# A decoder layer on one core: latent attention weights turned by 32x32 blocks on VectorE, and values times weights in tiles of 32 rows

## The chip, the core and the metric

The kernel runs on one core of a Trainium2 chip. The metric is device time in microseconds from launch to end, the median of several executions. Engines are named as the profile names them: PE is TensorE (PEld its weight loads), DVE is VectorE, ACT is ScalarE, POOL is GpSimd, SP is SyncE, whose queue issues nearly all DMAs here.

## What is computed

32 sequences of 256 tokens with 256 channels pass through one decoder layer, all in float32:

```python
x = layernorm(x + latent_attention(x))
x = layernorm(x + cross_attention(x, ctx))     # 16 heads of 64, 120 context rows
x = layernorm(x + experts(x) + shared(x))      # 16 experts, 32 tokens each, and a shared one

def latent_attention(x):                       # H = 16 heads, L = 72 latent columns
    kv = x @ latent_w + latent_b               # [b, 256, 72]: keys and values of every head
    q = einsum('btc,hcl->bhtl', x, Wd_w) + Wd_b
    scores = einsum('bhtl,bsl->bhts', q, kv) / sqrt(16)
    attn = softmax(where(causal, scores, -inf))
    y = einsum('bhts,bsl->bhtl', attn, kv)     # the product that the change is about
    return concat_heads(y) @ out_w + out_b     # 16 * 72 = 1152 columns into 256
```

Attention is causal: of 256 x 256 weights per head, the upper right quarter of 128 x 128 is never computed.

## The kernel before

The 32 sequences run one behind the other, as a pipeline written out by hand: `first_half(n)` and `second_half(n)` hold steps of sequence n (latent scores of four groups of four heads), n-1 (the weighting, `latent_out`, cross attention) and n-2, n-3 (the rest of cross attention, the routing). For n from 1 on, the order on PE and ACT is the order in which the code calls the steps; DVE, POOL and SP are ordered by the planner, which gives steps inside `urgent()` precedence. The last sequence overlaps the feed-forward part, which follows and whose steps come from a generator (`fill`).

The steps around the change, for group g of four heads:

- `scores` makes four PSUM tiles `pS` of 128 x 384: token block 0 against keys 0 to 127, and token block 1 against keys 0 to 255. The 72 latent columns are taken as 64 (row tiles of 64, L442) and 8 (row tiles of 32, L430). DVE adds the mask (L451) into `sm`.
- `weights` is the softmax in place: DVE maximum (L464), ACT exponent (L467), DVE reciprocal, POOL product (L475).
- `turn` transposes `sm` on PE (L489) in three blocks of 128 per head, 48 per sequence, into a PSUM tile `pT`; DVE (L493) or ACT (L495) copies it to `pt0` and `pt1`.
- `weigh` (L509) multiplies the 64 first value columns (the stationary operand, column tiles of 64, two heads side by side) with the turned weights, once per group, into `pz`; `weigh_rest` (L530) does the same with the last 8 columns, spread to 32, in column tiles of 32 (four heads side by side) for all groups into one `pzr`.
- Copies bring them to `zT`, nine chunks of 128 rows; `latent_out` multiplies these with `ow_sb` (18 matmuls of 256 columns, `po`), adds the residual and normalizes.

PSUM is eight banks: two with the tag "l" for cross scores and six with the tag "r" for all else, given out in rotation; a step that takes a bank waits until the copy out of its last use is done. An f32 matmul shows as two weight loads and two passes in the profile.

Of the kernel before, what the change touches and what calls it, by code (L numbers as in the profile page):

```python
# [26 lines left out]
P = 128  # L27
# [5 lines left out]
def decoder_kernel(  # L33
# [34 lines left out]
    HG = 4  # L68
# [10 lines left out]
    LR = L - LM  # L79
    QW = P // BQ  # L80
# [14 lines left out]

    mask = const.tile([P, 3 * P], F32, name="mask")
    nc.gpsimd.memset(mask, 0.0)
    for b in (0, 2):
        nc.gpsimd.affine_select(
            out=mask[:, b * P : (b + 1) * P],  # L100
            in_=mask[:, b * P : (b + 1) * P],
            compare_op=ALU.is_ge,
            fill=NEG,
            base=0,
            pattern=[[-1, P]],
            channel_multiplier=1,
        )
# [20 lines left out]

    VW = LM + NG * (32 + LR)

# [40 lines left out]
    def transposed(dst, src, name):  # L173

        turned = bank("r", [P, DC, T], name)
        for d in range(DC):
            for t in range(TC):
                nc.tensor.transpose(
                    turned[:, d, t * P : (t + 1) * P], src[:, t, d * P : (d + 1) * P], ident
                )  # L180
        with urgent():
            nc.vector.tensor_copy(dst, turned)
# [51 lines left out]
    v_bufs = [wp.tile([P, TC, VW], F32, name=f"v_{k}") for k in range(2)]  # L234
    for vb in v_bufs:
        nc.gpsimd.memset(vb, 0.0)
# [69 lines left out]
    def out_weights(part):  # L306
# [6 lines left out]
        for h in range(part * H // 2, (part + 1) * H // 2):  # L313
            lo = (h % HG) * 32 + (h // HG) * LR
# [16 lines left out]

    def load_context(m):
# [6 lines left out]
    def turn_x(s):  # L339
        st = states[s]  # L340
        st["xT"] = sp.tile([P, DC, T], F32, tag="xT", name=f"xT_{st['nm']}")
        transposed(st["xT"], st["x"], f"pxT_{st['nm']}")
# [20 lines left out]
    def values(s):  # L363
# [7 lines left out]
        v = v_bufs[s % 2]  # L371
        with urgent():
            nc.vector.tensor_copy(v[:, :, 0:LM], pv[:, :, 0:LM])
            nc.vector.tensor_copy(
                v[:, :, LM:].rearrange("p t (g k) -> p t g k", g=NG)[:, :, :, 0:LR],
                pv[:, :, LM:L].unsqueeze(2).to_broadcast([P, TC, NG, LR]),
            )
        st["v"] = v
# [98 lines left out]
    def turn(s, g, k):  # L477


        st = states[s]  # L480
        nm = f"{st['nm']}_{g}_{k}"
        if k == 0:
            st["pt0", g] = sp.tile([P, HG, TC, P], F32, tag="pt0", bufs=NG, name=f"pt0_{nm}")
        if k == 2:
            st["pt1", g] = sp.tile([P, HG, P], F32, tag="pt1", bufs=NG, name=f"pt1_{nm}")
        pT = bank("r", [P, HG, P], f"pT_{nm}")
        for j in range(HG):
            block = st["sm", g][:, j, k * P : (k + 1) * P]
            nc.tensor.transpose(pT[:, j, :], block, ident)  # L489
        dst = st["pt1", g] if k == 2 else st["pt0", g][:, :, k, :]  # L490
        with urgent():
            if k == 1:
                nc.vector.tensor_copy(dst, pT)  # L493
            else:
                nc.scalar.copy(dst, pT)  # L495

    def moving(st, g, j, k):
        return st["pt1", g][:, j, :] if k else st["pt0", g][:, j].rearrange("p t q -> p (t q)")

    def weigh(s, g):  # L500

        st = states[s]
        if g == 0:
            st["zT"] = sp.tile([P, ZC, T], F32, tag="zT", bufs=1, name=f"zT_{st['nm']}")
        pz = bank("r", [P, HG // 2, T], f"pz_{st['nm']}_{g}")
        for a in range(HG // 2):
            for k in range(TC):
                for odd in range(2):
                    nc.tensor.matmul(  # L509
                        pz[odd * LM : (odd + 1) * LM, a, k * P :],  # L510
                        st["v"][:, k, 0:LM],
                        moving(st, g, 2 * a + odd, k),
                        start=(k == 0),
                        stop=(k == TC - 1),
                    )
        dst = st["zT"][:, 2 * g : 2 * g + 2, :]
        with urgent():
            if g % 2:
                nc.vector.tensor_copy(dst, pz)
            else:  # L520
                nc.scalar.copy(dst, pz)

    def weigh_rest(s):

        st = states[s]
        pzr = bank("r", [P, T], f"pzr_{st['nm']}")
        for g in range(NG):
            for k in range(TC):
                for j in range(HG):
                    nc.tensor.matmul(  # L530
                        pzr[j * 32 : (j + 1) * 32, k * P :],
                        st["v"][:, k, LM + 32 * g : LM + 32 * (g + 1)],
                        moving(st, g, j, k),
                        start=(g == 0 and k == 0),
                        stop=(g == NG - 1 and k == TC - 1),
                    )
        with urgent():
            nc.scalar.copy(st["zT"][:, ZC - 1, :], pzr)

    def latent_out(s):  # L540
        st = states[s]
        po = bank("r", [P, TC, C], f"po_{st['nm']}")
        for t in range(TC):
            project(
                po[:, t, :],
                [(st["zT"][:, c, t * P : (t + 1) * P], ow_sb[:, c, :]) for c in range(ZC)],
            )
        r1 = ap.tile([P, TC, C], F32, tag="r", name=f"r1_{st['nm']}")
# [5 lines left out]
    def turn_x1(s):  # L554
        st = states[s]
        st["x1T"] = ap.tile([P, DC, T], F32, tag="xnT", bufs=1, name=f"x1T_{st['nm']}")
        transposed(st["x1T"], st["x1"], f"px1T_{st['nm']}")
# [3 lines left out]
    def cross_keys(m, n):  # L561

        pair = pairs[m]
        kxT = ap.tile([P, 4, 2, S2], F32, tag=f"kxT{n}", bufs=1, name=f"kxT_{m}_{n}")
# [743 lines left out]
```

## Time and profile before

| | |
|---|---|
| median of 3 runs | 3392.89 us (3392.28 to 3395.72) |
| the profiled execution | 3392.11 us, span of its instructions 3390.3 us |
| PE busy | 3368.9 us, 99% of the span |
| DVE, ACT, POOL busy | 1538.1, 1502.3, 1070.3 us |
| 800 to 1800 us (attention): DVE, ACT, POOL busy | 540, 564, 306 us of 1000 |
| granted PE clock | 1.00 |

Busy time of PE counts pipelined matmuls with their tails, so that 99% does not mean an array at its peak; the distance between the starts of two groups is what a group takes from the stream. A row of a group reads: line, engine, operation, written tile <- read tiles, shapes, count | busy us, mean ns of one | idle time before them and what ended it.

### The profile page before, as it was taken

The numbers are of one execution on the slowest core, as the hardware profiler recorded it, in microseconds if no ns is written. First come the engines' busy times: TensorE is split into PE (matmuls) and PEld (weight loads), VectorE is DVE, ScalarE is ACT, GpSimd is POOL, SyncE is SP. The second block draws the span as 40 slices with busy tenths as digits, with TensorE's granted clock in tenths as the row PEclk, the third lists the DMA queues.
The fourth block names the chain that finished last, engine by engine and source line by source line (L and its number), as shares of the span: only waits on it lengthen the run. The fifth ranks groups of instructions, "written<-read, shape, count | busy, mean of one in ns | idle before, by whom it ended". The sixth has DMA issues, their size and how long they took to land.

```text
span 3390.3 us, 59258 instructions
## 1 busy us (share of the span) xinstructions
PE 3368.9 (99%) x23020; PEld 2558.0 (75%) x23020; DVE 1538.1 (45%) x3416; ACT 1502.3 (44%) x5461; POOL 1070.3 (32%) x947
## 2 busy tenths in 40 slices
PE   9999999999999999999999999999999999999999
PEld 7788888888888888888888788887666655666655
DVE  4555555555555555555554655553322133121133
ACT  4656555555555555555555555564311111111111
POOL 3333333232322323232323223233444401444400
PEclk9999999999999999999999999999999999999999
DMA  3000000000000000000000000003455521555421
GB/s 99 11 17 26 15 22 18 17 19 22 21 18 19 19 16 25 18 21 19 15 20 15 27 17 21 16 12 111 108 124 124 135 90 57 122 124 123 103 86 47
DMA packets 142880, 164.50 MB, mean 49 GB/s; under 512 B 29448, under 2 KB 118536, under 8 KB 142600
## 3 DMA queue, kind: packets, MB, share of 16 engines
q1 hardware_dynamic: 117808, 126.08, 12.0%
q0 software_dynamic: 24576, 34.62, 5.7%
q8 instruction: 183, 3.00, 0.4%
q14 instruction: 97, 0.79, 0.1%
q10 hardware_dynamic: 216, 0.01, 0.0%
HBM read 105.61 MB, written 50.86 MB: 46 GB/s over the span
## 4 chain that ended last, share of the span: by engine, by line
PE 96%; DVE 2%; ACT 2%; POOL 0%; issue 0%; DMA 0%; SPq 0%; POOLq 0%; DVEq 0%; ACTq 0%
PE po L188 13%; PE pq L188 7%; PE pqx L188 7%; PE pd L188 7%; PE pu L188 6%; PE pg L188 6%; PE pS L442 5%; PE pz L509 5%; PE pT L489 5%; PE pc L667 3%; PE pu_s L188 3%; PE pg_s L188 3%; PE pL L625 3%; PE pfo L188 3%; PE pS L430 3%; PE pkx L188 3%
## 5 line engine op out<-in xcount | busy, mean ns | idle before, releaser
L475 POOL TENSOR_TENSOR sm<-sm,rs 128x512 f32<-128x512 f32 (+1 forms) x256 | 375.3, 1466 | 455.2 <-DVE rs L474 447.4
L467 ACT ACTIVATE sm<-sm,nmax 128x128 f32<-128x128 f32 (+1 forms) x1024 | 453.7, 462 | 89.2 <-DVE nmax L464 89.2
L475 POOL TENSOR_TENSOR xsm_x<-xsm_x,rs_x 128x480 f32<-128x480 f32 x256 | 252.1, 986 | 735.8 <-DVE rs_x L474 714.7
L467 ACT ACTIVATE xsm_x<-pL,nmax_x 128x120 f32<-128x120 f32 x1024 | 354.3, 375 | 13.2 <-DVE mv L160 10.2
L1082 POOL DMA_INDIRECT acc<-eo,offs x128 | 200.7, 1568 | 336.1 <-DVE eo L1079 295.0
L451 DVE TENSOR_TENSOR sm<-pS,mask 128x384 f32<-128x384 f32 x512 | 248.9, 547 | 90.0 <-PE pS L442 89.9
L188 PE MATMUL pq<-xT,wd_sb 128*128 128x256 f32 x1152 | 278.6, 383 | 0.5 <-DVE wd_sb L295 0.5
L188 PE MATMUL po<-ow_sb,zT 128*128 128x256 f32 x1152 | 257.1, 382 | 0.0
L188 PE MATMUL pqx<-x1T,wq_sb 128*128 128x256 f32 x1024 | 241.1, 384 | 2.2 <-ACT vx L594 0.8
L188 PE MATMUL pg<-xeT,wg 128*128 128x512 f32 x512 | 240.8, 593 | 0.0
L188 PE MATMUL pu<-xeT,wu 128*128 128x512 f32 x512 | 240.8, 593 | 0.0
L188 PEld LDWEIGHTS po<-ow_sb,zT 128*128 128x128 f32 x1152 | 216.8, 190 | 31.1
L1153 DVE TENSOR_TENSOR hT<-gl,pu 128x512 f32<-128x512 f32 x128 | 87.9, 687 | 334.0 <-PE pu L188 253.1
L188 PEld LDWEIGHTS pq<-xT,wd_sb 128*128 128x128 f32 x1152 | 211.7, 190 | 30.4 <-DVE wd_sb L295 0.9
L464 DVE TENSOR_REDUCE nmax<-sm 128x4 f32<-128x512 f32 (+1 forms) x256 | 231.2, 944 | 2.3
L188 PE MATMUL po<-wo_sb,cxT 128*128 128x256 f32 x1024 | 227.6, 381 | 0.0
L467 ACT ACTIVATION_READ_ACCUMULATOR xsm_x<-pL,nmax_x 128x1 f32 x1024 | 227.3, 222 | 0.0
L188 PE MATMUL pd<-wd,hT 128*128 128x256 f32 x1024 | 226.6, 380 | 0.0
L188 PEld LDWEIGHTS pqx<-x1T,wq_sb 128*128 128x128 f32 x1024 | 188.8, 190 | 38.3 <-issue 9.9
L474 DVE RECIPROCAL rs<-rs 128x4 f32<-128x4 f32 x256 | 45.4, 177 | 370.3 <-ACT sm L467 366.8
L467 ACT ACTIVATION_READ_ACCUMULATOR sm<-sm,nmax 128x1 f32 x1024 | 212.7, 208 | 0.0
L188 PEld LDWEIGHTS pd<-wd,hT 128*128 128x128 f32 x1024 | 192.6, 191 | 25.2 <-issue 1.0
(139 smaller groups left out, 6035.6 us busy)
## 6 DMA issues: line engine op xcount, KB each, us to landing
wg<-in_wg_dram SPq DMA_DIRECT2D x32, 512.0 KB
wu<-in_wu_dram SPq DMA_DIRECT2D x32, 512.0 KB
wd<-in_wd_dram SPq DMA_DIRECT2D x32, 512.0 KB
x<-in_x_dram SPq DMA_DIRECT2D x32, 256.0 KB
rows<-x SPq DMA_DIRECT2D x32, 256.0 KB
acc<-x SPq DMA_DIRECT2D x32, 256.0 KB
x2t<-x2T SPq DMA_DIRECT2D x32, 256.0 KB
fx2T_s<-x2t SPq DMA_DIRECT2D x16, 512.0 KB
```

Of the source, the lines that this page charges most:

```text
L188: nc.tensor.matmul(acc, lhsT, rhs, start=(i == 0), stop=(i == n - 1))
L430: nc.tensor.matmul(pS[j][:, SEG[t]], st["q8"][rows, t * P : (t + 1) * P], kr[rows, g, 0 : (t + 1) * P], start=(t == TC - 1), stop=False,)
L442: nc.tensor.matmul(pS[2 * a + odd][:, SEG[t]], st["qT", g][rows, a, t * P : (t + 1) * P], k[rows, 0 : (t + 1) * P], start=False, stop=(t = ...
L451: nc.vector.tensor_tensor(sm[:, j, :], pS[j], mask, ALU.add)
L464: nc.vector.tensor_reduce(nmax, src, AX.X, ALU.max, negate=True)
L467: nc.scalar.activation(dst[:, a, :], src[:, a, :], AF.Exp, bias=nmax[:, a : a + 1], accum_out=rs[:, a, :],)
L475: nc.gpsimd.tensor_tensor(dst, dst, rs.to_broadcast([P, n, width]), ALU.mult)
L489: nc.tensor.transpose(pT[:, j, :], block, ident)
L509: nc.tensor.matmul(pz[odd * LM : (odd + 1) * LM, a, k * P :], st["v"][:, k, 0:LM], moving(st, g, 2 * a + odd, k), start=(k == 0), stop=(k ...
L625: nc.tensor.matmul(pLs[odd][:, j, :], st["qxT", c0][rows, j, t * P : (t + 1) * P], pairs[s // 2]["kxT", c0][rows, j, s % 2, :], start=True ...
L667: nc.tensor.matmul(pc[odd * DH : (odd + 1) * DH, a, :], st["vx"][:, 2 * (c0 + j0 + a) + odd, :], st["xpt", c0, odd][:, j0 + a, :], start=True,
L1082: nc.gpsimd.indirect_dma_start(out=acc[b], out_offset=self.rows(b), in_=eo[:, k, :], in_offset=None, compute_op=ALU.add,)
```

## The change

- **Turning.** `turn` no longer uses PE. DVE transposes `sm` in blocks of 32x32, inside each set of 32 partitions, four instructions per group (two per token block, of 2 heads each), into tiles `d` that hold for each key block two odd/even sets of heads side by side. A weight of key k in block b then lies on the partitions of its *token's* 32-block, not of its key's: in `d` partition r*32+i holds key i of any key block, for the 32 tokens of token block r.
- **Weighing.** So for each set of 32 partitions (token block r) the contraction runs over 32 keys at a time, with the values of every key block on every set of 32 partitions. `weigh_half` does it for eight heads: matmuls of 32 rows by 64 columns with 128 moving columns (four heads of 32 tokens), eight different tiles of the array in turn, nine steps each; `weigh_rest` does the last 8 value columns of all 16 heads in tiles of 32 rows by 32 columns, sixteen of them, nine steps. Each r accumulates in a PSUM bank of its own.
- **Reversed blocks.** Token block r of the first half has r+1 key blocks below the diagonal. To give each set of partitions nine steps, the second half's four 32-token blocks come in reverse order: `xb` is a second load of these tokens, four DMAs, and the third part of the mask is changed to match. The copies out of PSUM put the blocks back in order.
- **Values.** `values` writes the 256 x 72 values to DRAM, and `place_values` reads them back four times, so that all eight key blocks lie on each set of 32 partitions.
- **The ninth chunk.** The last 8 columns now come as four chunks in which 8 of each 32 rows count; 16 DMAs of 8 rows each gather them into the chunk that `latent_out` reads.
- **Order.** `weigh` is called twice per sequence and not four times, `turn` of group 1 moves from the second half to the end of the first, `cross_keys` is cut into two parts around the cross weights, and `cross_values` of the second part moves to the second half. Buffers `r1`, `r2`, `x2` go from two to one.

```diff
-    for b in (0, 2):
-        nc.gpsimd.affine_select(out=mask[:, b * P : (b + 1) * P],
...
+    nc.gpsimd.affine_select(out=mask[:, 0:P],
...
+    for r in range(RB):
+        rows = slice(r * KB, (r + 1) * KB)
+        own = mask[rows, 2 * P :]
+        if r:
+            nc.gpsimd.memset(own[:, 0 : r * KB], NEG)
+        nc.gpsimd.tensor_copy(own[:, rows], mask[rows, rows])
...
+        st["xb"] = sp.tile([P, C], F32, tag="xb", bufs=1, name=f"xb_{s}")
+        for r in range(RB):
+            t0 = T - (r + 1) * KB
+            nc.sync.dma_start(out=st["xb"][r * KB : (r + 1) * KB, :], in_=x[s, t0 : t0 + KB, :])
...
-        transposed(st["xT"], st["x"], f"pxT_{st['nm']}")
+        transposed(st["xT"], (st["x"][:, 0, :], st["xb"]), f"pxT_{st['nm']}")
...
+            nc.vector.tensor_copy(v, pv)
+        st["v"] = dram.tile([P, TC, L], F32, tag="vd", bufs=2, name=f"vd_{st['nm']}")
+        nc.sync.dma_start(out=st["v"], in_=v)
+
+    def place_values(s):
+        by_block = states[s]["v"].rearrange("(b i) t l -> i b (t l)", i=KB)
+        for r in range(RB):
+            nc.sync.dma_start(
+                out=vals[r * KB : (r + 1) * KB, 0:VN].rearrange("i (b n) -> i b n", b=RB),
+                in_=by_block,
+            )
...
+    def turn(s, g):
+        st = states[s]
+        half, k = divmod(g, 2)
+        for t in range(TC):
+            nb = (t + 1) * RB
+            if k == 0:
+                st["d", half, t] = sp.tile(
+                    [P, nb, 2, HG, KB], F32, tag=f"d{half}{t}", bufs=1, name=f"d_{s}_{half}_{t}"
+                )
+            d = st["d", half, t][:, :, :, 2 * k : 2 * k + 2, :]
+            block = st["sm", g][:, :, SEG[t]]
+            for odd in range(2):
+                nc.vector.transpose(
+                    d[:, :, odd].rearrange("p b a i -> p a b i"),
+                    block[:, odd::2].rearrange("p a (b i) -> p a b i", i=KB),
+                )
+
+    def keys_of(r):
+        first = [(0, b, 2 * b) for b in range(r + 1)]
+        second = [(1, b, 2 * b) for b in range(RB)] + [(1, RB + b, 2 * b + 1) for b in range(r, RB)]
+        return first + second
+
+    def where(r):
+        return slice(r, 2 * RB - r, 2 * RB - 1 - 2 * r)
+
+    def weigh_half(st, pzs, half):
+        steps = [keys_of(r) for r in range(RB)]
+        for i in range(len(steps[0])):
+            for r in range(RB):
+                t, b, at = steps[r][i]
+                rows = slice(r * KB, (r + 1) * KB)
                 for odd in range(2):
                     nc.tensor.matmul(
+                        pzs[r][odd * LM : (odd + 1) * LM, t, 0 : HG * KB],
+                        vals[rows, at * L : at * L + LM],
+                        st["d", half, t][rows, b, odd].rearrange("p a i -> p (a i)"),
+                        start=(i == 0),
+                        stop=(i == len(steps[0]) - 1),
                     )
+
+    def weigh_rest(st, pzs):
...
                 for j in range(HG):
+                    half, odd = divmod(j, 2)
                     nc.tensor.matmul(
+                        pzs[r][j * 32 : (j + 1) * 32, t, HG * KB :],
+                        vals[rows, at * L + LM : at * L + LM + 32],
+                        st["d", half, t][rows, b, odd].rearrange("p a i -> p (a i)"),
...
+    def weigh(s, half):
...
+        n = HG * (1 + half)
+        pzs = [bank("r", [P, TC, n * KB], f"pz_{st['nm']}_{half}_{r}") for r in range(RB)]
+        weigh_half(st, pzs, half)
+        if half:
+            weigh_rest(st, pzs)
+        blocks_of = st["zT"].rearrange("p c (b i) -> p b c i", i=KB)
+        for r in range(RB):
+            dst = blocks_of[:, where(r), half * HG : half * HG + n, :]
+            src = pzs[r].rearrange("p t (c i) -> p t c i", i=KB)
+            with urgent():
+                if r % 2:
+                    nc.vector.tensor_copy(dst, src)
+                else:
+                    nc.scalar.copy(dst, src)
+        if half:
+            for j in range(HG):
+                for a in range(HG):
+                    lo = j * 32 + a * LR
+                    nc.sync.dma_start(
+                        out=st["zT"][lo : lo + LR, ZC + HG - 1, :],
+                        in_=st["zT"][j * 32 : j * 32 + LR, ZC - 1 + a, :],
+                    )
...
     def first_half(n):
+        odd = n % 2 and n > 1
         scores(n, 0)
...
-        turns(n - 1, 3)
+        run(turn, n - 1, 3)
...
-        run(weigh_rest, n - 1)
-        run(weigh, n - 1, 2)
-        run(weigh, n - 1, 3)
+        if odd:
+            cross_keys(n // 2, 0, (2,))
+        run(weigh, n - 1, 1)
+        if n:
+            place_values(n)
...
+        turn(n, 0)
...
+        turn(n, 1)
         run(cross_queries, n - 1, 0, 0)
         run(cross_queries, n - 1, 0, 2)
...
     def second_half(n):
...
-        turns(n, 1)
...
+        if odd:
+            run(cross_values, n - 1, 1)
...
         weigh(n, 0)
-        weigh(n, 1)
         run(cross_weigh, n - 2, 4)
...
-        turns(n, 2)
+        turn(n, 2)
...
+        else:
+            run(cross_values, n - 1, 1)
...
         values(0)
+        place_values(0)
         load_weights([(wk_sb, wk)])
```

## The prediction

> **What bounds the kernel now.** I read the page first: the span, the busy shares, and the chain that ended last.
>
> ```profile
> span 3390.3 us, 59258 instructions
> ...
> PE 3368.9 (99%) x23020; PEld 2558.0 (75%) x23020; DVE 1538.1 (45%) x3416; ACT 1502.3 (44%) x5461; POOL 1070.3 (32%) x947
> ...
> PE 96%; DVE 2%; ACT 2%; POOL 0%; issue 0%; DMA 0%; SPq 0%; POOLq 0%; DVEq 0%; ACTq 0%
> ```
>
> TensorE carries 96% of the chain, so a microsecond taken off its stream is a microsecond off the kernel, until another engine is late. Next the busy time in a stretch of attention, 800 to 1800 us (columns: busy us and instructions of PE, weight loads, DVE, ACT, POOL; clock; DMA share; GB/s).
>
> ```profile
> 800.00:1800.00 1000.00, 997.92 (x8425) 827.70 (x8425) 540.30 (x1208) 564.47 (x2208) 305.78 (x274) 1.00 0.07 20
> ```
>
> The next table has 660 `pT` transposes in this stretch; a sequence has 48, so these are 13.75 sequences of 72.7 us. Per sequence DVE works 39.3 us and ACT 41.1 us; the clock is full. The groups by shape give the prices:
>
> ```profile
> L489 PE MATMUL pT<-ident,sm 128*128 128x128 f32 x660 | 81.0, 273 | 0.0
> ...
> L464 DVE TENSOR_REDUCE nmax<-sm 128x4 f32<-128x512 f32 x55 | 37.4, 680 | 0.9
> ...
> L493 DVE COPY pt<-pT 128x512 f32<-128x512 f32 x55 | 37.1, 674 | 0.0
> ...
> L164 DVE TENSOR_SCALAR x<-r,mv,rstd 128x256 f32<-128x256 f32 x54 | 19.9, 410 | 20.7 <-POOL rstd L162 20.7
> ...
> L519 DVE COPY zT<-pz 128x512 f32<-128x512 f32 x27 | 18.2, 675 | 24.6 <-PE pz L509 24.6
> ```
>
> Then TensorE's timeline at the place of the change (start, length with the tail of the last one, line, tiles, count):
>
> ```profile
> 1058.38 1.47 PE L489 MATMUL pT<-ident,sm 128*128 128x128 f32 x12
> 1059.69 1.04 PE L651 MATMUL pxT<-ident,xsm_x 128*120 128x128 f32 x8
> ...
> 1062.82 2.81 PE L530 MATMUL pzr<-pt,v 128*32 128x256 f32 x64
> 1065.56 2.82 PE L509 MATMUL pz<-pt,v 128*64 128x256 f32 x32
> 1068.21 1.90 PE L667 MATMUL pc<-xpt,vx 120*64 120x256 f32 x16
> 1070.04 0.93 PE L430 MATMUL pS<-kr,q 32*128 32x256 f32 x16
> 1070.90 0.48 PE L442 MATMUL pS<-kT,qT 64*128 64x256 f32 x1
> 1070.91 0.48 PE L442 MATMUL pS<-kD,qT 64*128 64x256 f32 x1
> ...
> 1073.30 0.92 PE L188 MATMUL po<-ow_sb,zT 128*128 128x256 f32 x3
> ```
>
> The reader is to take the distance from one start to the next. Twelve transposes take 1.31 us, 109 ns for 128 columns with the array to itself. Each f32 matmul is two records: the 32 of `weigh_rest` are 64. Alone, its 32 passes of 256 columns and 32 of 128 would be 32 x (218 + 109) ns = 10.5 us; they took 2.74, so four column tiles run 3.8 times as fast as one. `pz`, two column tiles: 5.2 us alone, 2.65 taken, 2.0 times. L430, four row tiles: 2.6 alone, 0.86 taken, 3.0 times. Row tiles and column tiles each run side by side. No row has both at once, or more than four.
>
> **TensorE's part.** Removed per sequence: 48 transposes, 4 x 1.31 = 5.24 us; four `pz`, which run in twos of 2.65 us, 5.30; one `pzr`, 2.74. Together 13.28 us. Added: `weigh_half` has 9 steps x 4 row tiles x 2 column tiles = 72 matmuls of 128 columns, 144 passes per half, 288 in both; `weigh_rest` has 9 x 4 x 4 = 144 matmuls, 288 passes. The work grows: 576 passes x 109 ns are 62.8 us alone, and all depends on how many tiles run together. Bounds for the halves: eight together 3.92 us, four (the most any row shows) 7.85. For the rest: sixteen 1.96, eight 3.92, four 7.85. I take eight for the halves, because both kinds of tiling reach nearly their whole factor in the rows, and the middle of sixteen and eight, 2.94, for the rest. Three entries into another tile shape cost 0.1 each (`px2T` to `pzr` in this timeline is 0.2 where the pitch is 0.11). Sum 7.2 us, a gain of 6.1 us per sequence.
>
> How densely can the sequencer issue? The densest row is `pzr`, a weight load and a pass every 43 ns; at that rate 576 pairs take 24.8 us, 11.5 more than before. But `kT` and `kD` of L442, in two row tiles, start 10 ns apart, so 43 is what the array took and not a floor of issue.
> [...]
> [...]
>
> **VectorE and ScalarE.** Off DVE: four `pt` copies of 0.674, the odd `pz` copies, 2 x 0.675, and two `v` copies, 0.5: 4.5 us. On: per group four block transposes, two of 256 columns and two of 512, so eight of each. The trace has no DVE transpose. A floor is one element per cycle as in 128x256 at 0.41 and 128x512 at 0.68, 8.7 us; a ceiling is twice that, 17.5. I take the floor, since the reduction of 512 and the copy of 512 cost the same whatever they do. With two copies of 256 and two of 512 into `zT` (2.2) and one `v` copy (0.3), DVE comes to 39.3 - 4.5 + 11.2 = 46 us of some 67, 69%; at the ceiling 82%. It stays below TensorE. ACT loses eight copies of 0.587 and more and falls to 37 us. Both hide behind TensorE; if the cover is gone, each turn stands with its 2.2 us in DVE's queue before `nmax` of the next scores and before the copies that give PSUM banks back.
> `weigh` now holds four of six "r" banks until four copies are done (two of 0.69 on DVE, two of 0.59 on ACT, 1.4 us). `cross_weigh` covers them with 1.83 us on the other two. Uncovered it is 1.4 us per half, 2.8 per sequence.
>
> **The DMAs.** SP's queue gets per sequence 16 small DMAs that gather the fourth kind of `zT` row, four that place the values, one that writes them out, four of `xb`. `latent_out` waits for the 16 with its ninth chunk, and all of TensorE stands behind it. Their price is that of eight-row DMAs in SP's timeline:
>
> ```profile
> 21.36 2.29 SPq L315 DMA_DIRECT2D ow_sb<-in_out_w_dram  x6
> ```
>
> 0.38 us each, 6.1 for 16. Ahead of them the copies, 1.4; behind them a landing, which I put at 2 (a DMA's issue itself is 0.3 to 0.6 here; the first `x` is issued at 0.72 and transposed at 3.96, 3.2 later). Together 9.5 us. Cover on TensorE: 1.83 of `cross_weigh`, 3.26 of scores and cross scores, and 16 of the 36 passes of `latent_out` (7.87 us from the start of `po` to the next group), 3.5: 8.6 us. I count 1 us per sequence; the ends are 0, and 7 if the four value DMAs of 0.6 go first, each gather takes 0.53 as the first ones at L315 do, and landing is 3.2. `vals` themselves have half a sequence and cost nothing. The 16 stand before the load of the next `x` on SP; that load waits for `latent_out` anyway.
> At the start, four `xb` DMAs of 0.45 us stand before the weights on SP and the values' way through DRAM before `wk`: between 2 and 8 us once, I take 5. The reversed token blocks cost nothing in the loop: same matmuls, same mask width.
>
> **The sum.** Against the profiled execution (3392.1 us, 1.8 beyond its span, 0.8 below the median): 32 x (13.28 - 7.2 - 1.0) = 163 us off, 5 on: 3234. I say 3230.
>
> **Rivals.** (1) *The array takes four tiles at a time* where row and column tiles meet. Then 576 passes are 15.7 us, 16.0 with entries, 2.7 above the old 13.28; with the 1 us wait 3.7 x 32 + 5 = 123: 3515, slower. It decides from 13.0 us / 576 = 22.6 ns per pass, fewer than five tiles together; the wait alone moves that to 20.8 ns. For it: no row has more than four. Against: neither kind loses much alone. (2) *The gain comes and DVE or SP give it back*: turns half on the path (4.4 us) or gathers late by 4 more. 163 - 140 leaves 23, plus 5 at the start: 3375. For it: before, `pzr` already waited for a DVE copy now and then, up to 1.7 us. Against: DVE has a third of its time free. (3) *All sixteen run, nothing waits*: 6.2 us of work, 7.1 x 32 = 227 less 5: 3170. (4) *Issue binds* at 43 ns per pair: 3760.
>
> **Chances.** My case with (3) 0.62, own range 3165 to 3275; (2) 0.17, of which a part within 0.2%; (1) 0.15; (4) 0.06. 0.2% is what a measurement of this kernel tells from no change. Faster 0.76, same 0.03, slower 0.21. The range goes from 3165 to 3420: below it some 3 in 100, above it (4), most of (1).
>
> **What would show it.** `weigh_half` should start every 109 ns eight passes, and take about 2 us per half; at 4 us, (1) holds. `pT`, L493 and L495 are gone. DVE rises to about 46 us per sequence and transposes are at 0.4 and 0.7. `po` should stand still no longer than 1 us after its first 16 passes; a longer stop is the gathers. I am wrong if TensorE's idle time before `pz` or `po` sums to over 5 us per sequence, or if the passes need over 23 ns.

## The result and the profile after

The changed kernel takes 3780.9 us (median; 3777.4 to 3794.3) where the kernel before takes 3393.4 in the same comparison: 1.115 times as long, 95% interval 1.112 to 1.118. The forecast, 3230, has the wrong sign, and its range ended at 3420.

The page after, the lines that answer to those of before (span; busy time; granted clock in 40 slices; the blocks of the instruction queue; the chain):

```profile
span 3777.3 us, 86034 instructions
...
PE 3446.2 (91%) x35820; PEld 2545.5 (67%) x35820; DVE 1724.5 (46%) x3832; ACT 1380.1 (37%) x5237; POOL 1069.6 (28%) x952
...
PEclk8899998999999998999999998999999999999999
...
q8 instruction: 282, 4.62, 0.5%
...
PE 64%; DVE 13%; ACT 8%; POOL 8%; issue 5%; SPq 1%; DMA 1%; ACTq 0%; POOLq 0%; DVEq 0%
```

TensorE fell from 96% of the chain to 64%: DVE, ACT and POOL (the softmax and layer-norm steps) now carry 29% of it, and 5% is "issue", a wait for nothing that the profile shows. The clock, full before, has slices at 0.8. One stretch of attention, 800 to 1800 us, as before:

```profile
800.00:1800.00 1000.00, 882.93 (x11910) 706.56 (x11909) 539.79 (x1219) 435.93 (x1792) 261.78 (x235) 0.92 0.09 25
```

The costliest new groups by shape, and what PE waited for (total us, times, longest), both from 800 to 1800 us:

```profile
L554 PE MATMUL pz<-d,vals 32*32 32x128 f32 x3456 | 67.7, 337 | 41.4 <-issue 41.4
L511 DVE STREAM_TRANSPOSE d<-sm 128x512 f32<-128x512 f32 x94 | 64.3, 699 | 94.7 <-POOL sm L493 94.4
...
L511 DVE STREAM_TRANSPOSE d<-sm 128x256 f32<-128x256 f32 x94 | 36.3, 424 | 67.7 <-PE pz L554 38.4 <-POOL sm L493 29.3
```

```profile
PE px1T L182 <- DVE x L168: 41.5, 12, 5.9
PE pz L554 <- issue: 41.4, 33, 2.4
PE po L192 <- DMA zT<-zT: 19.5, 10, 2.7
```

Three stops, then: in the middle of `weigh_rest` for no visible reason, before `turn_x1` for the layer norm, and in `latent_out` for the gathers. TensorE's timeline of one second weighting (the `weigh` that ends with `weigh_rest`) shows the first of them:

```profile
1070.28 2.32 PE L537 MATMUL pz<-d,vals 32*64 32x128 f32 x144
1072.53 0.49 PE L554 MATMUL pz<-d,vals 32*32 32x128 f32 x28
1074.38 1.90 PE L554 MATMUL pz<-d,vals 32*32 32x128 f32 x128 [1.36 <-issue]
1078.12 2.82 PE L554 MATMUL pz<-d,vals 32*32 32x128 f32 x128 [1.84 <-issue]
1081.59 0.64 PE L554 MATMUL pz<-d,vals 32*32 32x128 f32 x4 [0.65 <-issue]
1082.16 3.68 PE L724 MATMUL pc<-xpt,vx 120*64 120x256 f32 x16
```

`weigh_half` runs as forecast: 144 passes from 1070.28 to 1072.53, 2.25 us. Then TensorE stops, runs 128 passes, stops, runs 128, stops. 128 passes and 128 weight loads are 256 instructions, and the instruction queue brings just such blocks: 4.62 MB in 282 of them is 16.4 KB each, 64 bytes an instruction if one holds 256. The counts agree: TensorE's 2 x 35820 loads and passes are 279.8 times 256, for 282 blocks, and the kernel before has 2 x 23020, 179.8 times 256, for 183 (`q8 instruction: 183, 3.00, 0.4%` on its page). The queue's records in the trace end here at 1072.93, 1076.73 and 1080.22; TensorE goes on 1.37 to 1.45 us after each. From 1072.93 to 1080.22 are two blocks in 7.3 us, one per 3.7 us. In 20 sequences all 57 stops inside `weigh_rest` end 1.27 to 1.60 us after such a record. Where one stop follows another, the 3.7 us are on average 1.2 from TensorE's going on to the start of the next block's record, 1.0 for the record and 1.4 to the end of the stop.

The last row shows the second loss: `cross_weigh`, which in the kernel before took 1.83 us from its start to that of the next group, takes 3.61 here. The windows say why (the clock is the third number from the end):

```profile
1077.50:1080.00 2.50, 1.88 (x101) 1.70 (x102) 0.00 (x0) 0.00 (x0) 0.00 (x0) 0.50 0.02 7
...
1082.16:1085.77 3.61, 3.61 (x19) 1.71 (x17) 1.38 (x2) 0.00 (x0) 0.00 (x0) 0.50 0.12 33
```

**An account per sequence.** I took 20 sequences (from the `px1T` passes of the sixth to those of the 26th) in each trace, summed every distance over 0.5 us between the starts of two TensorE instructions, loads included, as a stop (such a distance contains the instruction's own 0.1 us), and the time at clock 0.5 outside of stops. What is left is the time per sequence, less the stops, less half of that slow time:

| run | us per sequence | stops | at half clock, outside stops | left |
|---|---|---|---|---|
| before | 73.35 | 0.17 | 0 | 73.2 |
| after | 84.94 | 12.23 | 10.89 | 67.3 |
| spread | 82.77 | 11.71 | 5.34 | 68.4 |
| cover | 82.59 | 10.57 | 8.38 | 67.8 |
| no gather | 85.49 | 13.02 | 10.24 | 67.4 |
| rest 2 of 9 | 77.18 | 9.22 | 5.00 | 65.5 |
| narrow | 84.94 | 13.14 | 10.52 | 66.5 |
| all three | 78.84 | 7.84 | 4.54 | 68.7 |
| wide output | 77.08 | 4.93 | 1.32 | 71.5 |
| spread more | 77.13 | 4.13 | 2.01 | 72.0 |
| 96 columns | 82.90 | 6.61 | 7.51 | 72.5 |
| 96, queries between | 76.36 | 4.45 | 1.00 | 71.4 |

The rows after the second are the runs described below. TensorE's own work did become shorter by 5.9 us (5.2 if the 0.1 us in each stop is put back). 12.2 us of stops and 5.4 us of half speed came in its place: 84.94 - 73.35 = 11.6 a sequence, 371 of the 388 us. The stops after are, per sequence, 4.5 inside `weigh_rest`, 3.6 before `px1T`, 2.1 in `latent_out`, 1.0 in `weigh_half` and just ahead of it (0.8 of it for a bank that DVE's copy of `xpt` gives back), 1.0 elsewhere.

### The profile page after: what moved, and what is told of

Same layout as the page of the kernel before. It is cut to its first block, busy times and chain, and to the rows that moved or that the text cites. A ratio compares the mean times of both kernels' runs of the same rounds, so it can differ in the third digit from the quotient of the medians.

```text
span 3777.3 us, 86034 instructions
## 1 busy us (share of the span) xinstructions
PE 3446.2 (91%) x35820; PEld 2545.5 (67%) x35820; DVE 1724.5 (46%) x3832; ACT 1380.1 (37%) x5237; POOL 1069.6 (28%) x952
## 3 DMA queue, kind: packets, MB, share of 16 engines
q8 instruction: 282, 4.62, 0.5%
## 4 chain that ended last, share of the span: by engine, by line
PE 64%; DVE 13%; ACT 8%; POOL 8%; issue 5%; SPq 1%; DMA 1%; ACTq 0%; POOLq 0%; DVEq 0%
PE pqx L192 6%; POOL sm L493 6%; PE pd L192 6%; PE pu L192 6%; PE pg L192 6%; PE pz L554 5%; PE pq L192 4%; DVE d L511 4%; PE pc L724 4%; ACT sm L485 4%; PE pz L537 4%; PE pg_s L192 3%; PE pu_s L192 3%; PE pfo L192 3%; PE pS L460 3%
## 5 line engine op out<-in xcount | busy, mean ns | idle before, releaser
L511 DVE STREAM_TRANSPOSE d<-sm 128x256 f32<-128x256 f32 (+1 forms) x512 | 273.9, 562 | 443.7 <-POOL sm L493 338.4
L192 PE MATMUL po<-ow_sb,zT 128*128 128x256 f32 x1152 | 287.9, 408 | 65.2 <-DMA zT<-zT 62.7
L192 PEld LDWEIGHTS po<-ow_sb,zT 128*128 128x128 f32 x1152 | 230.0, 204 | 113.8 <-issue 64.2
L554 PE MATMUL pz<-d,vals 32*32 32x128 f32 x9216 | 183.5, 340 | 115.4 <-issue 115.4
L192 PE MATMUL pq<-xT,wd_sb 128*128 128x256 f32 x1152 | 279.8, 384 | 1.0 <-DVE wd_sb L301 1.0
L192 PE MATMUL pqx<-x1T,wq_sb 128*128 128x256 f32 x1024 | 257.5, 402 | 0.8 <-DVE x1T L186 0.8
L554 PEld LDWEIGHTS pz<-d,vals 32*32 32x32 f32 x9216 | 129.8, 117 | 160.6 <-issue 151.1
L192 PEld LDWEIGHTS pqx<-x1T,wq_sb 128*128 128x128 f32 x1024 | 200.8, 204 | 33.1 <-DVE x1T L186 1.8
```

Of the source, the lines that this page charges most:

```text
L192: nc.tensor.matmul(acc, lhsT, rhs, start=(i == 0), stop=(i == n - 1))
L511: nc.vector.transpose(d[:, :, odd].rearrange("p b a i -> p a b i"), block[:, odd::2].rearrange("p a (b i) -> p a b i", i=KB),)
L554: nc.tensor.matmul(pzs[r][j * 32 : (j + 1) * 32, t, HG * KB :], vals[rows, at * L + LM : at * L + LM + 32], st["d", half, t][rows, b, odd] ...
```

## The experiments: how instructions arrive

**Spread.** The pieces of the second weighting are set apart by one query step and one cross-value step.

```diff
-        run(weigh, n - 1, 1)
+        if n > 1:
+            weigh(n - 1, 1, [(0, lambda: queries(n, 1)), (5, lambda: cross_values(n - 1, 0))])
```

> The dense stretch of the second weighting is thinned: after weigh_half come queries(n, 1) (8 passes of 256 columns, 1.7 us), then steps 0 to 4 of weigh_rest, then cross_values(n-1, 0) (4 passes of 512, 1.9 us), then steps 5 to 8. Same matmuls, another order. Theory A (TensorE's instructions come in blocks of 256 that arrive at one per 3.7 us, so 864 instructions in a row run dry; the idle time then lets the clock fall): the stops inside pz (5.3 us per sequence) shrink below 1.5, the clock in the loop rises from 0.92 to 0.95 or more, time 3480 to 3620 us. Theory B (sixteen tiles of 32x32 do not run side by side): the 288 passes of the rest take their 9.6 us wherever they stand, time 3760 to 3800.

Measured: 3720.9 us, between the two figures. The stops inside `weigh_rest` fell from 4.5 to 1.6 us a sequence (1.1 more now lie in the cross-value passes between its pieces), but the weighting then ends later, and the gathers with it: the stop in `latent_out` grew from 2.1 to 4.3. The sum of stops hardly moved, 12.2 to 11.7; the 60 us came of less time at half speed.

**Rest 2 of 9.** Seven of nine rounds of `weigh_rest` are left out.

```diff
     def weigh_rest(st, pzs):
...
-        steps = [keys_of(r) for r in range(RB)]
+        steps = [keys_of(r)[::8] for r in range(RB)]
```

> weigh_rest does two of its nine steps (the weights of most keys are left out of the last 8 value columns): 448 of 576 instructions of the rest go. Theory A: 416 instructions in a row are 1.6 blocks, the stops inside pz fall from 5.3 to under 1 us per sequence, cross_weigh and scores behind them run at the full clock again: 3430 to 3520. Theory B: seven ninths of the 9.6 us go and nothing else: 3780 - 32 x 7.5 = 3540, the clock behind it as before.

Measured: 3539.2, above the range of theory A and at the figure of theory B. The stops and the clock went theory A's way: inside `weigh_rest` 0.9 us of stops are left, and the time at half speed outside of stops fell from 10.9 to 5.0 us. Again `latent_out` takes some back: 5.0 us, since the 16 transfers now have less to hide behind. The time alone would also fit passes that are merely slow; the next run tells these apart.

**Narrow.** As many instructions, a quarter of the columns in 7 of 9 rounds.

```diff
+                na = 1 if b else HG
                 for j in range(HG):
...
-                        pzs[r][j * 32 : (j + 1) * 32, t, HG * KB :],
+                        pzs[r][j * 32 : (j + 1) * 32, t, HG * KB : (HG + na) * KB],
...
-                        st["d", half, t][rows, b, odd].rearrange("p a i -> p (a i)"),
+                        st["d", half, t][rows, b, odd, 0:na].rearrange("p a i -> p (a i)"),
```

> The changed kernel, with 7 of the 9 rounds of weigh_rest streaming 32 columns in place of 128: as many instructions, 42% of that step's streaming, output wrong in those columns (part of the rest rows' sums is left out). Fetch theory (the second weighting is limited by how fast instructions arrive, about 29 ns for a load and a pass, whatever they stream): within 25 us of the changed kernel, 3755 to 3800, and the stops between pz passes on issue stay near 40 us per 1000. Work theory (sixteen tiles share TensorE and are slower together than the sum said): 3560 to 3680, as leaving those passes out altogether gave 3539.

Measured: 3784.3, 3 us from the changed kernel. What the passes stream does not matter here; that there are so many does. PE's waits in the same stretch, with 41.4 before the edit:

```profile
PE pz L555 <- issue: 52.2, 33, 2.5
```

Between stops too the pitch is the same: 12.2 ns from pass to pass with 128 columns, 11.6 with mostly 32 (means outside of half speed, distances over 200 ns left out).

**A burst, and the burst spread.** The kernel before, with 256 tiny pairs of load and pass that belong to nothing, once in one place and once in eight.

```diff
+        for k in range(4 * lo, 4 * hi):
+            r = k % 4
+            rows = slice(32 * r, 32 * r + 32)
+            nc.tensor.matmul(
+                pb[rows, 0:32], ident[rows, 0:32], ident[rows, 0:32], start=True, stop=True
+            )
...
         run(weigh, n - 1, 3)
+        burst(n, 0, 32)
```

> The kernel before, and nothing of the change: in each sequence, after the second weighting, 256 more loads and 256 more tiny passes (32x32 weights, 32 columns, on the four tiles of the diagonal) in one burst whose result nobody reads. Work alone, at the 12.6 to 16 ns a pair of the changed kernel's stretches without a stop: 3.2 to 4.1 us and an entry of 0.3, 31 x 3.5 to 4.4 = 3500 to 3530, and no stops. Fetch theory: two more blocks of 256 instructions in one place, at one per about 3.7 us: one or two stops of 1 to 2 us on issue in each burst, 6 to 8 us a burst with them and up to 2 more by the half clock: 3580 to 3700.

> The same 512 instructions a sequence in the kernel before, as eight pieces of 64 at eight places of the sequence. Fetch theory: no stops, the clock at 1.0; only their issue, 3.2 to 4.1 us, and seven more entries at about 0.2: 4.6 to 5.8 us, 3535 to 3575, and below the burst in one place by 20 to 150. If instructions cost only their issue: above the burst in one place by the entries, 40 to 60 us.

Measured: 3579.2, 1 us under the range expected, and 3561.4, inside its range. In one place the burst stops once:

```profile
1077.89 1.97 PE L829 MATMUL pb<-ident 32*32 32x32 f32 x210
1082.56 0.86 PE L829 MATMUL pb<-ident 32*32 32x32 f32 x46 [2.70 <-issue]
```

19 stops in 20 sequences, 2.0 us a sequence, all on "issue", and 1.9 us a sequence at half speed outside of stops, in a kernel that has nothing else of the change. In eight places no such stop is left. That run is still only 18 us faster, less than the 20 to 150 expected, because its pieces wait for a PSUM bank that the cross softmax holds (1.65 us a sequence, a fault of where I put them), and TensorE's own work is 1.1 us longer, which eight entries into another tile shape would explain; that was not measured by itself. A pair takes 8.5 ns in both: so densely the sequencer issued here. 3.7 us per 256 instructions, 29 ns a pair, is how densely they arrived in the second weighting from its first stop on.

## The experiments: cover, gathers, clock

**Cover.** Cover is work of TensorE that runs while a result it needs later is being made. The cross keys and values that the change had moved away stand between `latent_out` and `turn_x1` again, and no longer where the change had put them.

```diff
-        both(cross_weights, n - 2, 4, 1)
+        run(cross_weights, n - 2, 4, 1, 0)
+        if odd:
+            cross_keys(n // 2, 0)
+        else:
+            run(cross_values, n - 1, 1)
+        run(cross_weights, n - 2, 4, 1, 1)
...
```

> Only the order of two steps of cross attention is put back: cross_keys (odd n) or the second cross_values (even n) stand again between latent_out and turn_x1, where the kernel before had them. Theory C (part of the loss is that nothing covers the layer norm between latent_out and turn_x1): the stop before px1T, 3.9 us per sequence, falls below 1, the passes behind it run at the full clock, time 3600 to 3690. If that stop is only a shadow of the stops before it (theory A alone), it moves elsewhere: 3750 to 3790.

Measured: 3717.3, 64 us less than the changed kernel, above the range expected. The stop before `px1T` fell from 3.6 to 1.0 us; `weigh_half`, which had lost what stood ahead of it, now waits 2.1 and not 1.0. In the kernel before, 1.31 us of `pT`, 1.73 of queries and 3.24 of cross keys stand between `po` and `px1T`:

```profile
1073.30 8.04 PE L188 MATMUL po<-ow_sb,zT 128*128 128x256 f32 x36
1081.17 1.47 PE L489 MATMUL pT<-ident,sm 128*128 128x128 f32 x12
1082.48 1.89 PE L188 MATMUL pq<-xT,wd_sb 128*128 128x256 f32 x8
1084.21 3.40 PE L188 MATMUL pkx<-c,wk_sb 128*128 128x240 f32 x16
1087.45 0.60 PE L178 MATMUL px1T<-ident,x 128*128 128x128 f32 x4
```

In the changed kernel only the queries are left:

```profile
1009.93 4.55 PE L192 MATMUL po<-ow_sb,zT 128*128 128x256 f32 x20 [1.88 <-DMA zT<-zT]
1014.32 1.89 PE L192 MATMUL pq<-xT,wd_sb 128*128 128x256 f32 x8
1019.55 1.14 PE L182 MATMUL px1T<-ident,x 128*128 128x128 f32 x4 [3.34 <-DVE x L168]
```

Lost cover is not all of this stop. The first step of the layer norm, DVE's addition `r`, starts 0.03 us after the end of `po` in the kernel before, and 1.85 us after it here, because a `turn` stands ahead of it in DVE's queue and waits for POOL's product. First the addition before, then DVE after:

```profile
1081.37 0.69 DVE L550 TENSOR_TENSOR r<-po,x 128x512 f32<-128x512 f32 x1 [1.92 <-PE po L188]
...
1015.10 1.31 DVE L511 STREAM_TRANSPOSE d<-sm 128x512 f32<-128x512 f32 x2 [2.01 <-POOL sm L493]
1016.33 0.65 DVE L604 TENSOR_TENSOR r<-po,x 128x512 f32<-128x512 f32 x1
```

Over the 20 sequences the addition starts 0.04 us after `po` before and 1.8 us after it in the changed kernel; the DVE instruction just ahead of it is a turn in all 20, and in 14 the addition is more than 0.5 us late. No run tried another order on DVE.

**No gather.** The 16 transfers, which in the changed kernel SP issues in 10.8 us, are left out; `latent_out` reads one of the four chunks instead. Their row in SP's timeline of the changed kernel:

```profile
997.70 10.78 SPq L586 DMA_DIRECT2D zT<-zT  x16
```

> The 16 gathering DMAs are left out and latent_out reads the first of the four ungathered chunks (so the last 8 value columns of most heads are missing from the result). The stop of po on these DMAs, 2.0 us per sequence, goes: 3700 to 3720 us if it stands alone, down to 3660 if the clock gains by it; no change (3770 to 3790) if the layer norm or something else is late by as much.

Measured: 3789.5, no gain. The stop in `latent_out` is gone, and the one before `px1T` went from 3.6 to 6.2 us: TensorE reaches the layer norm's wait earlier and waits longer there. The addition now starts 4.5 us after the end of `po` and not 1.8, in all 20 sequences behind a turn that waited for POOL.

**All three** edits at once.

> Spreading (3720.9), covering the layer norm (3717.3) and leaving the gathers out (3789.5) in one kernel. The one part left out of the computation is the gather (the output projection reads ungathered rows). Theory A (TensorE's work is as short as the sum said, about 66 us a sequence, and everything above it is stops that follow one another plus the half clock that they bring, so that taking one away only shows the next): the three together save far more than the sum of the single savings (60 + 64 + 0 = 124, which would be 3665), because no later stop is left to take the time up: 3350 to 3560. Theory B (savings add): 3640 to 3690. Theory C (the passes themselves are slower than the sum said): 3600 or more, with the mean clock near 1.0.

Measured: 3594.6. The single savings were 60, 64 and -9; together they save 186. So a stop that is taken away alone is in part, or wholly, paid at the next one. It missed 3350 to 3560 by 35: the layer norm's stop is back at 4.0 us although its cover is there, since the addition starts 4.6 us after `po`, behind the turn.

**A stop by itself.** The kernel before; one of the nine chunks of `zT`, now multiplied last, reaches the output projection over four transfers in a chain, in the second run over six (`range(1, 6)`).

```diff
+            nc.sync.dma_start(out=hop[0], in_=st["zT"][:, 7, :])
+            for k in range(1, 4):
+                nc.sync.dma_start(out=hop[k % 2], in_=hop[(k - 1) % 2])
...
```

> The kernel before, and nothing of the change: one of the nine rows of zT reaches the output projection by four transfers one after another, so that TensorE stops once in a sequence, by my estimate 2 to 4 us (four transfers at 2.2 against 6.5 of cover). Clock theory: a stop of 2 us and more is followed by a stretch of 3.4 to 10 us at half speed, so a sequence lengthens by the stop and by 1.5 to 3.5 on top, mean clock 0.95 to 0.98: 3394 + 32 x (stop + 1.5 to 3.5). If the half speed of the changed kernel comes of its dense passes (or of anything but stops): clock 1.0 and 3394 + 32 x stop.

> As the run with four transfers in a row (3425.0: its stops were 0.6 to 1.5 us and brought no half speed, one of 2.7 us did), now with six: at about 1.95 us a transfer the stop grows to 4 to 5 us in every sequence. Clock theory (a stop of more than about 2.5 us is followed by a stretch of 3.4 to 6.8 us at half speed, each costing half its length): 3394 + 31 x (4 to 5 + 1.7 to 3.4) = 3570 to 3655, mean clock 0.95 to 0.98. If the half speed needs dense passes as well: clock 1.0 and 3394 + 31 x (4 to 5) = 3520 to 3550.

Measured: 3425.0 and 3607.0. The first made stops of 0.5 to 3.1 us, three quarters of them under 1.6, with 0.2 us a sequence at half speed, and decided nothing. In the second every stop is over 3 us:

```profile
1005.46 3.72 PE L188 MATMUL po<-ow_sb,zT 128*128 128x256 f32 x16
1014.40 1.22 PE L188 MATMUL po<-ow_sb,hop 128*128 128x256 f32 x2 [5.22 <-DMA hop<-hop]
1015.41 5.51 PE L188 MATMUL po<-ow_sb,zT 128*128 128x256 f32 x16
```

Sixteen passes of the same shape take 3.7 us ahead of the stop and 5.5 behind it. Per sequence 4.8 us of stops and 4.1 at half speed, 4.8 + 2.1 = 6.8, x 31 = 212; measured 214 above its own kernel before (3392.6). So stops alone are enough for the half speed. In the 20 sequences of each of the 17 traces, lone stops (no other within 5 us ahead and 3 behind) and how many had half speed within 3.6 us of their end:

| stop, us | under 1 | 1 to 1.6 | 1.6 to 2 | 2 to 2.4 | 2.4 to 3 | over 3 |
|---|---|---|---|---|---|---|
| followed by half speed | 1 of 290 | 7 of 101 | 8 of 131 | 20 of 49 | 31 of 34 | 141 of 147 |

All 345 stretches at half speed began during a stop or at most 2.8 us after one; they last 3.4, 6.8 or 10.2 us (in the changed kernel 14, 10 and 16 of 40). By the table a stop of over 2.4 us is nearly always enough, 172 of 181. Two shorter ones close together can be: in the weighting shown above the clock falls during the second of two stops of 1.36 and 1.84 us.

## The experiments: versions

**Wide output**: spread and cover, and in place of the 16 transfers six more output matmuls with the output weights in four chunks that have zero rows between. **Spread more**: also the turns of the cross weights between the pieces of the weighting, one of them into a PSUM bank of the other tag.

```diff
-                    (st["zT"][:, c if c < ZC - 1 else ZC + HG - 1, t * P : (t + 1) * P], ow_sb[:, c, :])
-                    for c in range(ZC)
+                    (
+                        st["zT"][:, c, t * P : (t + 1) * P],
+                        ow_sb[:, c, :] if c < ZC else ow4[:, c - ZC, :],
+                    )
+                    for c in range(ZC - 1 + HG)
...
+        pT = bank("l" if (c0, t) == (0, 1) and s < B - 2 else "r", [S2, HG, P], f"pxT_{nm}")
...
+            (0, lambda: (queries(n, 1), run(cross_turn, n - 2, 0, 1, 0))),
+            (3, lambda: run(cross_turn, n - 2, 0, 1, 1)),
+            (6, lambda: cross_values(n - 1, 0)),
```

> Spread and cover as in the sum, and in place of the sixteen gather transfers six more output passes of 256 columns per sequence (the output weights of the rest rows are laid out in four chunks with zero rows between). Complete. Theory A: the sum's time plus 32 x 6 x 0.24 = 46 us, 3400 to 3610. If the zT evacuation itself is late (a wait of po for zT that no transfer causes): as much as the kernel with spread and cover and the gathers would give, 3620 to 3680.

> The same, with the two turns of the cross weights (eight passes of 0.30 us) also put between the pieces of the second weighting, so that its 864 instructions lie in about 11.7 us of work where e7 has 9.3 and one block of 256 per 3.7 us needs 12.5. Fetch theory: 30 to 120 us below e7, 3300 to 3550; faster than the kernel before only if all stops go. If the stops come from elsewhere or the turns' evacuation delays cross_weigh by as much: within 20 us of e7 or above.

Measured: 3531.0 and 3539.7. The six matmuls are twelve passes and cost 2.6 us a sequence where I had 1.4, and still the run is faster than the one without gathers (3594.6): with longer work ahead of it, the stop before `px1T` is 1.3 and not 4.0. Spreading further removed all but 1.2 of 1.9 us of the stops in the weighting:

```profile
1060.46 3.12 PE L542 MATMUL pz<-d,vals 32*64 32x128 f32 x144
1063.50 1.99 PE L192 MATMUL pq<-xT,wd_sb 128*128 128x256 f32 x8
...
1065.86 1.49 PE L559 MATMUL pz<-d,vals 32*32 32x128 f32 x96
...
1067.86 1.81 PE L559 MATMUL pz<-d,vals 32*32 32x128 f32 x96
```

and gained nothing, where 30 to 120 us were expected if the stops set the time: the stop before `px2T` grew from 1.1 to 1.5, and TensorE's own work by 0.5; that this is the entries into another tile shape, one for each piece, was not measured.

**96 columns**: with cover and wide output, but without spread, one pass weighs main and rest rows together (`LV` is 96 columns), half as many instructions. Then the same with **one engine to a bank** in the evacuation (the copies out of PSUM; the line with `copy`), and on top of it with **the queries between** weighting and scores in both halves.

```diff
+                        pzs[r][0:LV, t, odd * HG * KB : (odd + 1) * HG * KB],
+                        vals[rows, at * L : at * L + LV],
...
+                    copy = nc.vector.tensor_copy if r % 2 else nc.scalar.copy
...
         run(cross_weigh, n - 2, 4)
+        run(queries, n + 1, 0)
         scores(n, 3)
```

> Complete. From the changed kernel, with the cover of the layer norm put back and six more output passes in place of the gathers: main and rest rows of a token block are weighed by one pass with 96 columns of weights (64 main, 8 rest, 24 that meet zero rows), four tiles of 32 rows at once; 288 passes a sequence in place of 576, at most 288 instructions in one go; sixteen evacuations in place of four to six per weighting. My sum: 288 passes at 27 to 36 ns = 7.8 to 10.4 where the kernel before spends 13.3, 2.6 for the output passes: 0.3 to 2.9 us a sequence below the kernel before if nothing stops, 3300 to 3385. If the stops come of something other than the number of instructions, or the evacuations hold up the output projection: 3420 to 3600.

> The run with 96 columns of weights, with one edit: each bank of the weighting is evacuated by one engine (banks 0 and 2 by ScalarE, 1 and 3 by VectorE) and not by both in turn, which its trace shows waiting for each other (0.92 and 0.82 us of idle time before every second copy, 6.6 us for four banks). By copies of 0.36 to 0.42 us each engine then needs 3.2 us, the stop of the next scores (2.4 us, twice a sequence, with slow passes after it and half the clock after some) falls to about 1: 2 x (1.5 to 3) us a sequence, 3520 to 3620. If the stop is of the clock or of instructions: 3690 to 3715.

> The same, with the four query passes of 1.5 us put ahead of the scores in both halves, so that the banks come free before the scores ask for them. What is left above TensorE's work is then the wait of the second weighting for a bank (1.8 us a sequence) and up to 0.5 us before turn_x1: my sum is 72.6 - 13.3 + 8.7 (weighting) + 2.6 (output passes) + 2.3 = 72.9 a sequence, the kernel before within 1.5%: 3360 to 3460. If the scores' delay starves VectorE and the softmax chain: 3480 to 3600.

Measured: 3714.5, 3542.7 and 3513.7 (1.035 times before, 1.033 to 1.037). The first is above both ranges expected. The passes cost what I had worked out, 28.5 ns each with four tiles at once, and hardly a stop on "issue" is left inside the weighting. In the first run the scores wait for banks (4.4 us of stops a sequence, and 7.5 at half speed), because ACT and DVE take turns at one bank, each waiting for the other:

```profile
1058.39 0.36 ACT L562 COPY zT<-pz 32x256 f32<-32x256 f32 x1 [0.92 <-DVE zT L561]
1058.78 0.36 ACT L561 COPY zT<-pz 64x256 f32<-64x256 f32 x1
```

One engine to a bank took 172 us off, within its range; the order took 29 more, 54 us short of the range expected: the stop of the scores went, from 1.5 us a sequence to none, and the one before `px1T` grew from 0.6 to 2.4, having lost the queries as its cover. The third run has 4.5 us of stops left, 1.8 of them in the second weighting for a bank that DVE's copy of `xpt` gives back late. Without stops and half speed it would be at 71.4 us a sequence, 1.8 below before: an estimate from the table, which no run reached. No version here beats the kernel before.

## Why the prediction was wrong, point by point

- **TensorE's work: right.** Forecast 6.1 us a sequence less; 5.2 to 5.9 measured. Eight tiles do run together: 14.9 ns from pass to pass in the halves (forecast 13.6). Sixteen run at 12.2 ns (forecast 10.2); as the narrow run has nearly the same pitch, it is not the streaming that sets it. What does stays open, since the tiny pairs start 8.5 ns apart. Rival (1) is refuted.
- **"How densely can the sequencer issue?": the step that failed first.** I asked how fast instructions are issued and not how fast they arrive. 43 ns a pair was indeed no floor of issue, as I said: pairs start 8.5 ns apart in the burst and 12.2 in `weigh_rest`. What binds is the arrival: one second weighting is 432 pairs, 864 instructions, 3.4 blocks at 3.7 us each. That is 12.5 us for 5.7 of work (144 x 14.9 and 288 x 12.2 ns); the one in the timeline took 11.9, and the stops are 4.5 us a sequence. Rival (4), 3760, came near in time by luck: its mechanism, issue at 43 ns a pair, is not what the traces show.
- **The clock: left out.** I took full clock as given because before had it. The stops brought 10.9 us a sequence at half speed, 5.4 us lost.
- **The order of steps: left unpriced.** I priced the `pT` that goes from TensorE's stream, and not that 1.3 us of it, with 3.2 us of cross keys, had covered the layer norm. That stop is 3.6 us a sequence; the cover alone, put back, takes 2.6 of it away.
- **The gathers: dearer than my upper price.** I took 0.38 us each on SP and 0.53 at most; they took 0.67, 10.8 for 16. The stop is 2.1, not 1.0, and far from the upper end of 7. Taking it away alone gains nothing, as the run without them shows: it delays TensorE ahead of the next stop.
- **VectorE and ScalarE: right in load, not in order.** Transposes 0.42 and 0.70 us (floor 0.41 and 0.68); 539.8 and 435.9 us in 1000 / 84.94 = 11.8 sequences are 45.9 and 37.0 us, forecast 46 and 37. They did not come to bind by their load. I had the turns standing in DVE's queue ahead of `nmax` and of the copies out of PSUM, at 2.2 us each and hidden; a turn that waits for POOL's product also stood ahead of the layer norm's addition and made it 1.8 us late, 4.5 without the gathers.
- **What would prove me wrong** was named: more than 5 us of idle time before `pz` and `po`. It was 4.5 + 1.0 + 2.1 = 7.6.
- The start's 5 us and the reversed token blocks were not tried by themselves; some 17 of the 388 us lie outside the sequences' steady rate.

## What to carry to other kernels

Before a long product is cut into small tiles, count instructions as well as columns. A block of 256 came every 3.7 us here, 14 ns an instruction: 864 instructions in a row that came closer than that stopped here, first after 344 of them in the timeline above, and with other work between their pieces the stops in `weigh_rest` fell from 4.5 to 1.6 us a sequence. When a step leaves an engine's stream, ask what it had covered besides its own cost; when it enters another engine's queue, ask what stands behind it there and how long it may wait. A stop taken away alone can be paid at the next one: the 2.1 us in `latent_out` went, and the one before `px1T` grew from 3.6 to 6.2. A stop of over 2.4 us of TensorE nearly always cost more than its length here (172 of 181 lone ones), since passes behind it ran at half speed.

## What the runs showed of the hardware that I had not expected

- Instructions reached TensorE in blocks of 256 (282 blocks for 279.8 times 256 instructions), one per 3.7 us while it waited for them in the second weighting, of which the transfer itself is 1.0; it issued a load and a pass in 8.5 ns in the burst.
- Half speed followed lone stops of over 2.4 us in 172 of 181 cases, in stretches of 3.4, 6.8 or 10.2 us, also where nothing but a wait is new (4.1 us a sequence with six transfers in a chain).
- Passes on sixteen tiles of 32x32 started 12.2 ns apart with 128 columns, and 11.6 with mostly 32.
